# One more buffer for gathered rows, three instead of four groups projected beside the table, and a looser pacing of gathers, in a graph attention layer on one core

## The chip, the cores and the metric

The kernel runs on one core of a Trainium2 chip. The metric is the device time of one execution in microseconds (us), and of several executions the median counts. In this text PE (or TensorE) is the matrix engine and PEld its weight loads, DVE (VectorE) and ACT (ScalarE) are the two elementwise engines, POOL (GpSimd) here does little but start indirect gathers, and SP starts most of the direct transfers.

## The reference

A graph attention layer with a residual, a batch normalization over the nodes and a layer normalization, on 12,500 nodes and 212,500 edges that are sorted by their destination. Cut to what matters:

```python
Q = (x @ WQ).reshape(N, H, dh)          # N = 12500, D = 128, H = 8 heads of dh = 16
K = (x @ WK).reshape(N, H, dh)
V = (x @ WV).reshape(N, H, dh)
Eh = (edge_attr @ WE).reshape(-1, H, dh)
score = K[src] * Q[dst] / jnp.sqrt(jnp.float32(dh)) * Eh
score = jnp.exp(jnp.clip(score.sum(-1, keepdims=True), -5.0, 5.0))
msg = V[src] * score
wV = jax.ops.segment_sum(msg, dst, num_segments=N)
Z = jax.ops.segment_sum(score, dst, num_segments=N)
h = x + (wV / (Z + ATTN_EPS)).reshape(N, D)
h = (h - h.mean(0)) * rsqrt(var(h) + BN_EPS) * gamma + beta
out = layernorm(x + h)
```

Everything is float32.

## The kernel before

**Edges, tiles and groups.** The edges are cut into 1661 tiles of 128 edges, and the tiles into 208 groups of up to 8 (`G`). A group is the unit of the main loop. Its two halves of four tiles each write into one window of 64 destination nodes. The order of the instructions on every engine is the order in which the program is written (`manual_schedule`); no planner moves them. Only waits on data and on buffers decide when they run.

**The table of K and V.** `K[src]` and `V[src]` are rows of a table `kvd` in DRAM, 12,500 rows of 256 numbers (1 KB). The program builds it first: 25 steps of `table_rows` (L656 to L676), each for four blocks of 128 nodes: eight projections with `w_kv` (L663), evacuations that alternate between ScalarE and VectorE (`evac`, L306 and L307), and one write on SP's queue (L671). The first preparations of the main loop (one-hot matrices, queries, edge attributes of groups 0 to 2) are spread over the last steps, written out by hand in the list `steps`. `q_window(w)` reads two node numbers into ScalarE's registers and copies the x columns of the two windows of group w (L497).

**Gathers on POOL.** Groups from 8 (`nxg`) on take their table rows with indirect gathers: one instruction of POOL (L225) for one tile, 128 rows of 1 KB; a group's eight make a set. A set lands in one of 8 slots (`NSLOT`), tiles of the pool `rows`. The list `free` names the free slots and `pending` the groups that still want one; `load_kv` (L279) pairs them and puts the gathers into `queued`. It is called where a slot comes free: after `message(g)` (L603), the last reader of group g's rows, and after the projection of the groups below.

A gather that is queued is issued at one place of an iteration of the main loop: `pace(step)` (L237) issues the first and makes it wait for the product of that iteration that has just been written (`add_x`, L643, or `q_mm`, L528); `issue()` sends the rest behind it.

**The first eight groups.** They can't wait for the table. POOL gathers rows of x for them (64 gathers of 128 rows of 512 bytes), two groups in one slot, called a pair slot here. The rows are transposed (`turn_x`, L322) and projected (`project`, L329) by the kernel itself. `EARLY` = 4 groups are projected beside the table, in two pieces of four tiles each, into slots of their own; the other four in the main loop (`project_main`, L480, with all copies on ScalarE), one per iteration and one iteration ahead of their use, into the table's buffers `t`. Of the x gathers 11 start at once, and the rest are paced by the table: after each step those that are due wait for one of its evacuations (L675).

**Rows fetched on SP.** To relieve POOL, the last tile of 24 groups doesn't come by a gather but by single transfers of one row (1 KB) on SP's queue (`fetch_rows`, L277). There are 3072 of them, spread 16 to an iteration from iteration 8 (`FIRST_ROW`) to 199. On the same queue stand the group's edge attributes `ea` (L477, 512 KB, four iterations ahead) and the node numbers of the one-hot matrices.

**An iteration of the main loop** (L767 to L813) for group g writes in this order: `load(g+4)` of `ea`; `fetch_rows(g)`; `products(g)` (L579, rows times queries); `both_halves(g+1)` (L560); `add_x(g-3)` and `q_mm(g+3)` with the paced gathers; `gather_sum(g-1)` (L618, the segment sums on TensorE); `project_main(g+1)` for the first groups; `turn_back(g+1)` (L568); `scores(g)` (L585); the exponential; `ehqe(g+2)` (L547 the projection of `ea`, L549 its evacuation, L555 the queries); `message(g)` (L603); `onehot(g+1)` (L508). After iteration 7 the table's pool is closed (`tps.close()`), and a new pool `late` takes its memory, for the tiles that the fetched rows land in. After the loop the nodes are normalized and written out.

Of the kernel before, what the change touches and what calls it, by code (L numbers as in the profile page):

```python
# [8 lines left out]
F32 = mybir.dt.float32  # L9
# [8 lines left out]
P = 128  # L18
# [3 lines left out]
G = 8  # L22
# [2 lines left out]
CH = 512  # L25
NSLOT = 8
NX = 8
EARLY = 4
RUN = 64
ROWS = P  # L30
FIRST_ROW = 8
# [51 lines left out]
def gnn_kernel(  # L83
# [33 lines left out]
    rows = ctx.enter_context(tc.tile_pool(name="rows", bufs=1))  # L117
# [6 lines left out]
    late = []  # L124
# [16 lines left out]
    nxg = min(NX, sum(k == G for k in sizes))  # L141
# [9 lines left out]
    def load_xT(upto):  # L151
        while loaded[0] < min(upto, N):
            c = loaded[0]
            n = min(512 if c < 1024 else 1024, N - c)
            nc.sync.dma_start(hx[:, c:c + n], xT[:, c:c + n])
            loaded[0] += n
# [53 lines left out]
    free = list(range(NSLOT))  # L210
    pending = list(range(nxg, NG))
# [1 line left out]
    steady = [False]  # L213

    def slot(i):
        return rows.tile([P, 2 * G * P], F32, name=f"slot{i}")

    def kv_view(g, t):
        SLOT[g] = t[0]
# [9 lines left out]
    queued = []  # L229

    def issue(n=0):
        while len(queued) > n:
            f, *a = queued.pop(0)
            f(*a)
# [13 lines left out]
    for (_, n), groups in zip(ROW_STREAMS, row_plan(usizes)):  # L248
# [6 lines left out]
        if tot % n:  # L255
            q = tot // n
# [22 lines left out]
    def load_kv():  # L279
        while free and pending and table[0]:  # L280
            g = pending.pop(0)
            i = free.pop(0)
            kv_view(g, (i, slot(i)))
            for j in range(sizes[g] - (g in by_row)):
                queued.append((gather, KV[g](j, j + 1, 0, 2 * P).rearrange("p a d -> p (a d)"), kvd,
                               starts[g] + j))
            if not steady[0]:
                issue()
# [46 lines left out]
    def within(f, g):  # L335
        return f(g) if 0 <= g < NG else None


    runs = []
# [151 lines left out]
    def q_window(g):  # L491
        _, BASE[g] = nc.values_load_multi_w_load_instructions(
            base_i[0:1, 2 * g:2 * g + 2], engines=(ET.Activation,), min_val=0, max_val=N,
            skip_runtime_bounds_check_because="node ids")
        XW[g] = wp.tile([P, P], F32, name="xw", bufs=8)
        for h in (0, 1):
            nc.scalar.activation(XW[g][:, h * WN:(h + 1) * WN], hx[:, ds(BASE[g][h], WN)], AF.Copy)  # L497
# [158 lines left out]
    def table_rows(b):  # L656
        t = tab.tile([P, 4, 2 * P], F32, name="t", bufs=4)
        for q in range(b, min(b + 4, NB), 2):
            ps = wide()
            m = min(2, NB - q)  # L660
            for i in range(m):
                n = min(P, N - (q + i) * P)
                nc.tensor.matmul(ps[:n, i, :], hx[:, (q + i) * P:(q + i) * P + n], w_kv, start=True, stop=True)  # L663
            fl = min(m, N // P - q)
            if fl:
                step = evac(t[:, q - b:q - b + fl, :], ps[:, :fl, :])
            if fl < m:
                nc.vector.tensor_copy(t[:n, q - b + fl, :], ps[:n, fl, :])
        full = min(4, N // P - b)
        if full > 0:  # L670
            nc.sync.dma_start(kvd[b * P:(b + full) * P, :].rearrange("(c p) d -> p c d", p=P), t[:, :full, :])  # L671
        if b + 4 > N // P and N % P:
            r0 = N // P * P
            nc.sync.dma_start(kvd[r0:N, :], t[:N - r0, N // P - b, :])
        while len(queued) > max(0, nxg * G - 11 - 11 * (b // 4 + 1) // 5):  # L675
            pace(step)  # L676

    NQ = -(-NB // 4)
    early = min(EARLY, nxg)
    piece = {}  # L680
    for k in range(2 * early):
        piece.setdefault(3 + k * (NQ - 4) // (2 * early), []).append((k // 2, 4 * (k % 2)))
    def both_halves(g):
# [1 line left out]
        both(g, 1)  # L685


    steps = [[(locate,)], [(place, runs[0])], [(q_window, 0), (q_window, 1)], [(q_mm, 0), (q_hi, 0)],
             [(q_mid, 0), (load_rel, 0)], [(q_lo, 0), (load, 0)], [(q_mm, 1), (q_hi, 1), (load_rel, 1)],
             [(q_mid, 1), (q_window, 2)], [(q_lo, 1), (load_rel, 2)], [(load, 1)], [(turned_onehot, 0)],  # L690
             [(turned_onehot, 1)], [], [(ehqe, 0), (both_halves, 0)], [(turn_back, 0), (q_mm, 2), (q_hi, 2)],
             [(q_mid, 2)]]
    first_step = NQ - len(steps) - 1
    assert first_step > 3 and max(piece) < first_step + 14
    for q in range(NQ):
        load_xT((q + 5) * 4 * P)
        if q == 2:
            load_rest()
        for g, a in piece.get(q, []):
            if a == 0:  # L700
                i = free.pop(0)
                kv_view(g, (i, slot(i)))
            turn_x(g, a)
        table_rows(4 * q)
        for g, a in piece.get(q, []):
            project(g, a, wide)
        k = q - first_step
        if 0 <= k < len(steps):
            for f, *a in steps[k]:
                f(*a)  # L710
# [47 lines left out]
    def within_checks(g):  # L758
        if g >= first_check and (g - first_check) % every == 0:
            check((g - first_check) // every)  # L760
# [6 lines left out]
    for g in range(NG - 2):  # L767
        within(load, g + 4)
        within(load_rel, g + 5)
        if (g + 6) % RQ == 0 and (g + 6) // RQ in quads:  # L770
            load_quad((g + 6) // RQ)
        fetch_rows(g)
        within(products, g)
        within(both_halves, g + 1)
        step = within(add_x, g - 3)
        step = within(q_mm, g + 3) or step
        if step is not None and queued:
            pace(step)
        issue()
        within(gather_sum, g - 1)  # L780
        if g + 1 < nxg and g + 1 not in SLOT:
            for _ in project_main(g + 1):
                pass
        within(turn_back, g + 1)
        within(scores, g)
        within(clip_exp, g)
        within(q_hi, g + 3)
        within(x_out, g - 3)
        within(sums_out, g - 1)
        within(q_lo, g + 2)  # L790
        within(denom, g - 2)
        within(recip, g - 2)
        within(attn, g - 2)
        within(q_window, g + 4)
        within(turned_onehot, g + 3)
        within(ehqe, g + 2)
        within(q_mid, g + 3)
        within(message, g)
        within(onehot, g + 1)
        if g == 2:  # L800
            load_last()
        for r in runs[1:]:
            if g == max(4, r[0] // 2 - 12):
                place(r)
        within_checks(g)
        while free and todo and not pending:
            load_x()
        bn_parts(2 * g - 5, 2 * g - 3)
        if g == 4:
            nc.vector.tensor_scalar(row_ids, row_ids, 8 * P, None, op0=OP.mult)  # L810
        if g == FIRST_ROW - 1:
            tps.close()
            late.append(tps.enter_context(tc.tile_pool(name="late", bufs=1)))  # L813
    last = NG - 1
    g = last - 1
    assert not any(k >= g for k in fill)
# [5 lines left out]
    step = add_x(g - 3)  # L822
# [320 lines left out]
```

## Time and profile before

| | |
|---|---|
| median of 3 runs | 2701.23 us (2698.18, 2701.23, 2709.0) |
| the profiled execution, its own time | 2704.18 us |
| its span, first to last instruction | 2702.4 us |
| mean granted TensorE clock | 0.826 |
| PE, DVE, POOL, ACT busy | 71%, 61%, 58%, 24% of the span |
| indirect gathers of table rows on POOL (L225) | 1573, 948 ns each |
| one-row fetches on SP's queue (L277) | 3072, 1 KB each |
| DMA packets, bytes | 177,915; 386.83 MB |

The durations below are those of the profiled execution. A line of a timeline gives the start in us from the span's beginning, the duration in us, the engine, the source line, the operation with its output and inputs, the number of instructions in a row that the line stands for, and in brackets how long the engine was idle before and what released it. `remote` there is a releaser that the profile can't name, and `issue` means that the engine waited for nothing that the profile shows. In a table of costly groups, the columns are busy time with the mean in ns, and then the idle time before, with the wait that ended most of it.

### The profile page before, as it was taken

Reading aid. Unit: us, or ns where it says so; the run is one execution under the profiler, and the core shown is the slowest. Engines: PE = TensorE matmul, PEld = TensorE weight load, DVE = VectorE, ACT = ScalarE, POOL = GpSimd, SP = SyncE. Lnnn points to the kernel's source line nnn. Section 1 sums busy time; section 2 is a strip of 40 time slices with the busy share of each in tenths; the row PEclk is TensorE's granted clock in tenths of the full one; section 3 lists DMA queues with packets and bytes.
Section 4 is the critical chain, followed back from the end, with each engine's and each line's share of the span. In section 5 each row is a group of like instructions: output and inputs, shape, how many; then the busy total and the mean of one; then the engine's idle time right before and its main releaser. Section 6 shows DMA issues by size and latency. Waiting matters only on the chain. (4 is left out here: it accounts for less than half of the span.)

```text
span 2702.4 us, 37686 instructions
## 1 busy us (share of the span) xinstructions
PE 1926.2 (71%) x9414; PEld 1144.2 (42%) x9414; DVE 1644.1 (61%) x3598; ACT 658.4 (24%) x2477; POOL 1579.8 (58%) x1673
## 2 busy tenths in 40 slices
PE   7787766767777767667675767667777767677677
PEld 5454433433434434334333444334344434444446
DVE  3456665565666565666554665656656656656577
ACT  2242222222222222222221222222222222222225
POOL 5645665565666666565654666665656665656624
PEclk8888888887888878888777888878778887878899
DMA  7744444444454444454444544444544444544454
GB/s 225 237 138 139 139 133 143 127 145 135 136 144 141 135 140 141 129 151 130 141 139 117 145 134 135 139 140 130 146 134 140 141 141 132 149 133 140 141 174 127
DMA packets 177915, 386.83 MB, mean 143 GB/s; under 512 B 38864, under 2 KB 94713, under 8 KB 177689
## 3 DMA queue, kind: packets, MB, share of 16 engines
q0 software_dynamic: 77552, 210.48, 26.8%
q1 hardware_dynamic: 95972, 171.08, 20.8%
q10 hardware_dynamic: 4163, 2.79, 0.3%
q8 instruction: 77, 1.26, 0.2%
q14 instruction: 151, 1.22, 0.1%
HBM read 364.58 MB, written 19.63 MB: 142 GB/s over the span
## 5 line engine op out<-in xcount | busy, mean ns | idle before, releaser
L225 POOL DMA_INDIRECT slot<-kvd,srcs x1573 | 1491.1, 948 | 1002.3 <-PE ps_m L528 469.5
L547 PE MATMUL ps_e<-ea,w_e 128*128 128x512 f32 x832 | 640.4, 914 | 528.7 <-DMA ea<-eaT 455.1
L560 DVE TENSOR_TENSOR wt<-wt,ps_q 128x512 f32<-128x512 f32 x416 | 267.6, 682 | 501.1 <-PE ps_q L555 153.5
L618 PE MATMUL ps_a<-msg,oh 128*128 128x136 f32 (+1 forms) x3322 | 516.8, 293 | 9.6 <-issue 8.8
L547 PEld LDWEIGHTS ps_e<-ea,w_e 128*128 128x128 f32 x832 | 207.9, 276 | 738.9 <-issue 719.7
L549 ACT ACTIVATE wt<-ps_e 128x512 f32<-128x512 f32 x416 | 243.1, 595 | 1024.9 <-PE ps_e L547 374.9
L618 PEld LDWEIGHTS ps_a<-msg,oh 128*128 128x128 f32 (+1 forms) x3322 | 415.6, 167 | 88.9 <-issue 61.6
L579 DVE TENSOR_TENSOR p<-slot,ps_t 128x512 f32<-128x512 f32 (+1 forms) x408 | 263.3, 671 | 172.0 <-PE ps_e L547 86.0
L568 PE MATMUL ps_t<-ident,wt 128*128 128x128 f32 x1661 | 248.2, 294 | 130.0 <-DVE wt L560 94.5
L568 PEld LDWEIGHTS ps_t<-ident,wt 128*128 128x128 f32 x1661 | 202.1, 150 | 152.4 <-DVE wt L560 107.3
L585 DVE TENSOR_REDUCE s<-p 128x64 f32<-128x1024 f32 (+1 forms) x209 | 251.7, 1204 | 0.2
L594 ACT ACTIVATE ps_m<-s 128x64 f32<-128x64 f32 (+1 forms) x209 | 47.5, 227 | 823.2 <-DVE s L593 468.7
L603 DVE TENSOR_TENSOR msg<-slot,ps_m 128x1024 f32<-128x1024 f32 (+1 forms) x206 | 243.2, 1182 | 0.6 <-ACT ps_m L594 0.6
L555 PE MATMUL ps_q<-ot,q 64*128 64x512 bf16 x1248 | 220.0, 469 | 0.0
L555 PEld LDWEIGHTS <-q 64*128 64x128 bf16 x1248 | 50.6, 106 | 294.0 <-issue 280.3
L508 DVE TENSOR_TENSOR oh<-ps_m,rel_i 128x512 f32<-128x512 f32 x208 | 141.7, 681 | 10.0 <-remote 8.6
L643 PE MATMUL ps_m<-ident,at 128*128 128x128 f32 x412 | 109.9, 352 | 41.4 <-DVE oh L511 22.3
L643 PEld LDWEIGHTS ps_m<-ident,at 128*128 128x128 f32 x412 | 70.1, 214 | 153.5 <-issue 88.6
L579 DVE TENSOR_TENSOR p<-byrow,ps_t 128x128 f32<-128x128 f32 x24 | 6.9, 286 | 157.7 <-DMA byrow<-kvd 118.2
L497 ACT ACTIVATE xw<-hx 128x64 f32 x416 | 84.1, 248 | 62.3 <-issue 58.0
L648 ACT ACTIVATE hx<-ps_m 128x64 f32 x412 | 90.8, 220 | 11.4 <-PE ps_m L644 3.3
L528 PE MATMUL ps_m<-w_q,xw 128*128 128x128 f32 x416 | 82.8, 282 | 10.3 <-issue 8.6
(167 smaller groups left out, 1625.6 us busy)
## 6 DMA issues: line engine op xcount, KB each, us to landing
ea<-eaT SPq DMA_DIRECT2D x207, 512.0 KB
byrow<-kvd SPq DMA_DIRECT2D x3072, 1.0 KB
slot<-kvd,srcs POOLq DMA_INDIRECT x1573
rbq<-relT SPq DMA_DIRECT2D x94, 256.0 KB
kvd<-t SPq DMA_DIRECT2D x24, 512.0 KB
slot<-xT SPq DMA_DIRECT2D x24, 256.0 KB
out<-o SPq DMA_DIRECT2D x23, 256.0 KB
hx<-xT SPq DMA_DIRECT2D x11, 512.0 KB
```

The source lines that it names most:

```text
L225: return nc.gpsimd.indirect_dma_start(out=out, out_offset=None, in_=table, in_offset=bass.IndirectOffsetOnAxis(ap=srcs[:, e:e + 1], axis=0))
L508: nc.vector.tensor_tensor(one, iota_ps[:, None, :].to_broadcast([P, n, P]), r[:, :n, None].to_broadcast([P, n, P]), op=OP.is_equal)
L547: nc.tensor.matmul(eh, w_e, EA[g][:, a:b, :].rearrange("p a b -> p (a b)"), start=True, stop=True)
L549: nc.scalar.activation(t[:, :(b - a) * P], eh, AF.Copy)
L555: nc.tensor.matmul(QE[g][h], Q3[g][r, k, :], OT[g][r, :(b - a) * P], start=(k == 0), stop=(k == 2))
L560: nc.vector.tensor_tensor(t, t, QE[g][h], op=OP.mult)
L568: nc.tensor.transpose(ps[:, j, :], WT[g][h][:, j * P:(j + 1) * P], ident)
L579: nc.vector.tensor_tensor(PR[g][:, c:d, :], KV[g](c, d, 0), PW[g][i][:, c - a:d - a, :], op=OP.mult)
L585: nc.vector.tensor_reduce(SS[g][:, a:b, :], PR[g][:, a:b, :].rearrange("p t (h d) -> p t h d", d=DH), axis=AX.X, op=OP.add)
L603: nc.vector.tensor_tensor(MSG[g][:, a:b, :P].rearrange("p t (h d) -> p t h d", d=DH), KV[g](a, b, P).rearrange("p t (h d) -> p t h d", d=D ...
L618: nc.tensor.matmul(AGG[g][WN if j >= n else 0:], OH[g][j], MSG[g][:, j, :], start=(j == 0), stop=(j == n - 1))
L643: nc.tensor.matmul(ps, AT[g], ident, start=True, stop=False)
```

## The change

- `EARLY` is 3: group 3 is no longer projected beside the table but in the main loop, like groups 4 to 7. The six pieces that are left are spread over the same steps.
- A ninth slot exists once the table's memory is free: at the end of iteration 7 slot number 8 is allocated from `late[0]`, put into `free`, and `load_kv` is called. Once no group is pending any more, the slot is taken out of `free` again, so that it isn't used for the reload of x at the end.
- The x gathers are paced by 12/5 instead of 11/5 per step of the table.
- The gathers that the main loop queues are paced only from iteration 8 on; before it all are issued without the wait.
- `q_window(0)` and `q_window(1)` are called at the beginning of table step 10 instead of its end, and `q_window(2)` at the beginning of step 16 instead of the end of step 15.

```diff
-EARLY = 4
+EARLY = 3
...
     def slot(i):
-        return rows.tile([P, 2 * G * P], F32, name=f"slot{i}")
+        return (rows if i < NSLOT else late[0]).tile([P, 2 * G * P], F32, name=f"slot{i}")
...
-        while len(queued) > max(0, nxg * G - 11 - 11 * (b // 4 + 1) // 5):
+        while len(queued) > max(0, nxg * G - 11 - 12 * (b // 4 + 1) // 5):
             pace(step)
...
-    steps = [[(locate,)], [(place, runs[0])], [(q_window, 0), (q_window, 1)], [(q_mm, 0), (q_hi, 0)],
+    steps = [[(locate,)], [(place, runs[0])], [], [(q_mm, 0), (q_hi, 0)],
...
-             [(q_mid, 1), (q_window, 2)], [(q_lo, 1), (load_rel, 2)], [(load, 1)], [(turned_onehot, 0)],
+             [(q_mid, 1)], [(q_lo, 1), (load_rel, 2)], [(load, 1)], [(turned_onehot, 0)],
...
+    windows = {first_step + 2: (0, 1), first_step + 8: (2,)}
     for q in range(NQ):
+        for w in windows.get(q, ()):
+            q_window(w)
         load_xT((q + 5) * 4 * P)
...
         step = within(q_mm, g + 3) or step
-        if step is not None and queued:
+        if step is not None and queued and g >= FIRST_ROW:
             pace(step)
         issue()
...
         within_checks(g)
+        if NSLOT in free and not pending:
+            free.remove(NSLOT)
         while free and todo and not pending:
             load_x()
...
         if g == FIRST_ROW - 1:
             tps.close()
             late.append(tps.enter_context(tc.tile_pool(name="late", bufs=1)))
+            free.append(NSLOT)
+            load_kv()
```

## The prediction, made before the changed kernel ran

> **What bounds the kernel now.** I read the page first, then the waits, then the timeline of single engines: SP's queue, POOL, and VectorE's score reductions (L585, one per group, so their starts are a clock of the groups). Page and waits:
>
> ```profile
> L225 POOL DMA_INDIRECT slot<-kvd,srcs x1573 | 1491.1, 948 | 1002.3 <-PE ps_m L528 469.5
> byrow<-kvd SPq DMA_DIRECT2D x3072, 1.0 KB
> PE ps_e L547 <- DMA ea<-eaT: 455.1, 135, 8.2
> ```
>
> No engine is full. TensorE's longest wait is for the edge attributes (`ea`), and those stand on SP's queue behind the 3072 one-row loads, 16 per group, so 192 rounds. SP's queue in the timeline:
>
> ```profile
> 210.89 0.33 SPq L477 DMA_DIRECT2D ea<-eaT  x1
> 214.43 5.24 SPq L277 DMA_DIRECT2D byrow<-kvd  x16
> ...
> 223.69 11.35 SPq L277 DMA_DIRECT2D byrow<-kvd  x16
> ...
> 2605.52 5.49 SPq L277 DMA_DIRECT2D byrow<-kvd  x16
> ```
>
> From the first round (214.4) to the end of the last (2611.0) are 2396.6 us, 12.5 us for each of 192 rounds, and SP issues nearly without pause. So the program is a head of 214 us, 192 rounds, and a tail of 91 us. Whatever moves the start of the first round moves the end by the same amount; what happens beside the rounds counts only if it changes a round.
>
> The same 16 loads take 5.2 us or 11.4 us. POOL tells which:
>
> ```profile
> 106.63 1.01 POOL L225 DMA_INDIRECT slot<-kvd,srcs  x1 [2.76 <-DMA rb<-relT]
> ...
> 135.44 0.95 POOL L225 DMA_INDIRECT slot<-kvd,srcs  x1 [0.30 <-issue]
> 140.88 0.94 POOL L225 DMA_INDIRECT slot<-kvd,srcs  x1 [4.49 <-PE ps_a L618]
> ...
> 149.77 0.94 POOL L225 DMA_INDIRECT slot<-kvd,srcs  x1 [0.30 <-issue]
> ...
> 203.84 0.94 POOL L225 DMA_INDIRECT slot<-kvd,srcs  x1 [15.49 <-PE ps_m L528]
> ...
> 212.60 0.94 POOL L225 DMA_INDIRECT slot<-kvd,srcs  x1 [0.30 <-issue]
> 223.00 0.94 POOL L225 DMA_INDIRECT slot<-kvd,srcs  x1 [9.46 <-PE ps_m L528]
> ...
> 231.76 0.95 POOL L225 DMA_INDIRECT slot<-kvd,srcs  x1 [0.30 <-issue]
> ```
>
> The round at 214.4 lies in POOL's pause from 213.5 to 223.0: 5 us. The one at 223.7 lies under eight gathers (223.0 to 232.7): 11 us. Gathers slow down what runs beside them. Eight take 10 us (140.88 to 149.77 and one more).
>
> A long row of gathers does more than slow down. Without a pause POOL ran from 106.6 to 136.4: 24 gathers, the sets of groups 8, 9 and 10. In that time:
>
> ```profile
> 116.60 1.21 DVE L603 TENSOR_TENSOR msg<-slot,ps_m 128x1024 f32<-128x1024 f32 x1
> 126.42 0.28 ACT L623 ACTIVATE os<-ps_a 128x136 f32<-128x136 f32 x1 [10.06 <-remote]
> 127.85 0.77 PE L528 MATMUL ps_m<-w_q,xw 128*128 128x128 f32 x2 [8.57 <-issue]
> ```
>
> and the score reductions:
>
> ```profile
> 105.19 1.21 DVE L585 TENSOR_REDUCE s<-p 128x64 f32<-128x1024 f32 x1
> 114.26 1.21 DVE L585 TENSOR_REDUCE s<-p 128x64 f32<-128x1024 f32 x1
> 142.29 1.21 DVE L585 TENSOR_REDUCE s<-p 128x64 f32<-128x1024 f32 x1
> 149.72 1.21 DVE L585 TENSOR_REDUCE s<-p 128x64 f32<-128x1024 f32 x1
> 166.21 1.22 DVE L585 TENSOR_REDUCE s<-p 128x64 f32<-128x1024 f32 x1
> 179.45 1.21 DVE L585 TENSOR_REDUCE s<-p 128x64 f32<-128x1024 f32 x1
> 192.36 1.21 DVE L585 TENSOR_REDUCE s<-p 128x64 f32<-128x1024 f32 x1
> 204.82 1.21 DVE L585 TENSOR_REDUCE s<-p 128x64 f32<-128x1024 f32 x1
> 216.47 1.21 DVE L585 TENSOR_REDUCE s<-p 128x64 f32<-128x1024 f32 x1
> 223.98 1.21 DVE L585 TENSOR_REDUCE s<-p 128x64 f32<-128x1024 f32 x1
> ```
>
> Group 1 to group 2 takes 28.0 us where group 0 to 1 took 9.1: 18.9 us are lost, and the groups go on at 139 us, three after the burst. The gathers of x beside the table show the same:
>
> ```profile
> 3.17 1.15 POOL L225 DMA_INDIRECT slot<-x,srcs  x1 [2.01 <-DMA srcs<-src]
> ...
> 23.36 0.94 POOL L225 DMA_INDIRECT slot<-x,srcs  x1 [0.30 <-issue]
> 27.92 0.94 POOL L225 DMA_INDIRECT slot<-x,srcs  x1 [3.62 <-ACT t L306]
> ...
> 97.61 0.94 POOL L225 DMA_INDIRECT slot<-x,srcs  x1 [3.04 <-DVE t L307]
> 19.36 0.60 ACT L306 ACTIVATE xt<-ps_t 128x512 f32<-128x512 f32 x1 [4.42 <-remote]
> 27.06 0.60 ACT L306 ACTIVATE t<-ps_e 128x512 f32<-128x512 f32 x1 [7.10 <-remote]
> 81.39 0.69 DVE L307 COPY t<-ps_q 128x512 f32<-128x512 f32 x1 [4.81 <-remote]
> ```
>
> 17 in a row (3.2 to 24.3) held ScalarE 4.4 + 7.1 = 11.5 us, until 27.1; the stop at 81.4 follows a shorter row. I take this as the rule of the case: about 10 us into a row of gathers the other engines stop, until about 3 us after its end. What the kernel calls pacing keeps sets apart.
>
> **The change, part by part.** The ninth slot. Sets are asked for some seven groups ahead: the 16 sets before the first round's 214 us are eight, for groups 8 to 15, and group 8's scores come at 216.5 although its gathers began at 106.6. No wait of a product for a slot stands among the long waits. Storing one set more ahead therefore hides nothing new: a set is still begun once per group, paced as before from group 8 on. Group 16's set moves one iteration forward, into the pause in which the first SP round took 5.2 us; that round may grow to 11.4 (+6.1), and at the end the gathers finish one iteration earlier, so one late round shrinks by as much. Net 0, ends -6 and +6. Its memory is the table's, free after group 7's message; the pool's other tiles were already placed there.
>
> The q windows. Windows 0 and 1 move from the end of a step of the table to its beginning, on ScalarE; window 2 keeps its place in ScalarE's order. Copies of 0.4 us, ends of -1 and 0; taken as 0.
>
> Three groups beside the table. One group fewer is two pieces fewer, each four transposes and eight products, with three copies on ScalarE or VectorE beside them. The products of one such piece and the share of each engine in the table's middle (us, then PE, PEld, DVE, ACT, POOL; clock, DMA share, GB/s), and a copy of a q window:
>
> ```profile
> 60.42 0.60 PE L322 MATMUL ps_t<-ident,slot 128*128 128x128 f32 x4
> 62.58 1.03 PE L329 MATMUL ps_q<-w_kv,xt 128*128 128x256 f32 x4
> 63.45 1.03 PE L329 MATMUL ps_e<-w_kv,xt 128*128 128x256 f32 x4
> 57.70 0.40 ACT L497 ACTIVATE xw<-hx 128x64 f32 x2 [1.03 <-issue]
> 50.00:100.00 50.00, 45.58 (x201) 36.80 (x202) 18.03 (x31) 15.40 (x34) 27.41 (x29) 0.91 0.82 266
> ```
>
> 2.66 us a piece, 5.3 for both; TensorE was busy 45.6 of the 50 us, so -4.8 if it sets the table's pace. The group is now projected in the loop, all on ScalarE. Groups 3 to 6 carry a projection (their next scores come 16.5, 13.2, 12.9, 12.5 us later, the first still recovering; mean of the last three 12.9), group 7 carries a gather set alone (11.7), and group 8 neither (7.5). So +1.2 if a set lies there too, +5.3 if none does; I take +3.1.
>
> Looser pacing of x. 53 of the 64 gathers are paced, 2.4 instead of 2.2 per step of four blocks; at 1.25 us each that is 3.0 instead of 2.75 us of POOL per step, and they are out two steps before the table ends. Rows of gathers grow longer: I allow three quarters of one more stop like that at 81.4, +3.5; ends 0 (nothing is added) and +9.6 (two stops). Table in sum: -1.3.
>
> No pacing before group 8. The sets of groups 8, 9 and 10 follow each other already. Set 11 waited 4.5 us for the paced matmul, and that pause ended the stop. Without it the slot is free (group 1's message ran at 116.6, before the stop bit), and set 11 follows at once: 32 gathers, 40 us. The stop lasts 10 us longer; beside group 7 a set that stands alone cost 11.65 - 7.51 = 4.1 us, which falls away. +5.9, ends 0 and +10. Then the pair 1 slot comes free in iteration 2 (group 3's projection, now in the loop) and group 2's slot in the same iteration, so sets 12 and 13 run as one row of 20 us instead of two of 10 with a pause. Price by the row nearest in length, the 17 gathers at the start: 11.5 us, less 8.2 for two single sets: +3.3; ends -8 and +11.
>
> Sum: -1.3 + 3.1 + 5.9 + 3.3 = +11.0 us. The profiled execution took 2704.2 us, span 2702.4 and 1.8 around it, 3.0 over the median of 2701.2; so 2715.2 for it, **2712 us** for the median. About 0.5% (13.5 us: 2687.7 and 2714.7) is what a measurement of this kernel tells from no change.
>
> **Rivals.**
> Gathers do not stop the engines. Then rows of any length are free, pacing cost nothing and its loss brings nothing: -4.8 + 3.1, 2699.5 us. This is what the Trainium skill states, in SBUF — State Buffer, section Who interferes with whom: DMA never contends with a compute engine, and PE and ACT never wait on anyone; by that rule alone the sum would have no burst term. The trace disagrees, with 10.06 us on ScalarE inside the 30 us burst. What speaks for this rival otherwise is that the waits end on a releaser the profile can't name; against it, three stops, each beside a row of gathers.
>
> The stop shrinks. From 97.6 us the x gathers ran almost into the kvd sets; in the new order POOL rests for the last two steps of the table. If the stop needs what the earlier gathers left behind, the engines run on longer before it bites: of 18.9 us it could take 14, and -1.7 from the first rival's terms: 2685.5 us. For it: at 116.6 VectorE was still on time, so a few us of delay let group 2 through. Against it: the burst itself gets longer.
>
> A second full stop (slower). Sets 12 and 13 start while the engines have just come back, and stop them as long as the first burst did: 18.9 instead of 11.5, set 11's stop costs its full 10, so -1.3 + 3.1 + 10 + 18.9 - 8.2 = +22.5: 2724 us. It decides from the point where set 13 follows set 12 without a pause while group 3 is still short of its scores. For it: both slots come free in one iteration. Against it: set 12 has to wait for TensorE to return, which gives a pause first.
>
> The change doing nothing it says: for the ninth slot that is my forecast already.
>
> **How the numbers follow.** Forecast 0.42 (0.27 within 0.5%, 0.15 beyond, since its terms reach from 2704 to 2722); first rival 0.14; the stop shrinks 0.23 (0.22 faster); second stop 0.21. Faster 0.22, within 0.5% 0.42, slower 0.36. The range takes in 2685.5 with its lower half cut, and the second stop with a table that got 10 us slower: 2684 to 2734.
>
> **What would show it.** Right: POOL in one row from about 105 to 145 us; group 1 to 2 in some 35 us; sets 12 and 13 in a row with another gap of over 15 us between scores; first SP round starting near 225 instead of 214; rounds of 12.5 us as before and the same tail. Wrong: the first round at 205 or earlier (the stop shrank), or a mean round other than 12.5 us, which would mean that the slot or the shifted sets act on the rounds, a thing for which I have no term: 0.1 us there is 19 us.

## The result, and the profile after

The changed kernel took 2731.58 us (median of 6 runs, 2729.0 to 2737.0), the kernel before 2708.30 us (6 runs, 2698.18 to 2712.51): a ratio of 1.0109, 95% interval 1.0089 to 1.0129. It is slower by about 1%, where 2712 was forecast. The profiled execution took 2731.76 us, 27.6 over the one before. Two of the costly groups on the page of the changed kernel:

```profile
L225 POOL DMA_INDIRECT slot<-kvd,srcs x1573 | 1492.0, 948 | 1018.1 <-issue 417.7
L547 PE MATMUL ps_e<-ea,w_e 128*128 128x512 f32 x832 | 628.5, 898 | 510.3 <-DMA ea<-eaT 478.2
```

The gathers are the same in number and length, and TensorE still waits longest for `ea`. SP's queue in the timeline of the changed kernel, its first and its last round of fetches:

```profile
238.36 10.22 SPq L277 DMA_DIRECT2D byrow<-kvd  x16
...
2628.76 5.54 SPq L277 DMA_DIRECT2D byrow<-kvd  x16
```

The head ends at 238.4 instead of 214.4 us (+23.9), the 192 rounds take 2395.9 instead of 2396.6 us (12.48 us each in both), and the tail takes 95.7 instead of 91.4 us (+4.3). So the division into head, rounds and tail holds, the rounds are untouched, and nearly all of the loss is in the head. Its steps, by the writes of the table (SP's queue, before and then after), the rows of gathers (POOL, after) and the starts of the groups' scores (VectorE, after):

```profile
101.57 0.41 SPq L674 DMA_DIRECT2D kvd<-t  x1
```
```profile
105.91 0.42 SPq L674 DMA_DIRECT2D kvd<-t  x1
```
```profile
109.64 0.95 POOL L225 DMA_INDIRECT slot<-kvd,srcs  x1 [6.76 <-issue]
...
148.54 0.95 POOL L225 DMA_INDIRECT slot<-kvd,srcs  x1 [0.30 <-issue]
156.19 0.94 POOL L225 DMA_INDIRECT slot<-kvd,srcs  x1 [6.71 <-PE ps_t L322]
...
174.95 0.94 POOL L225 DMA_INDIRECT slot<-kvd,srcs  x1 [0.30 <-issue]
194.44 0.94 POOL L225 DMA_INDIRECT slot<-kvd,srcs  x1 [18.55 <-PE ps_t L322]
...
219.78 0.94 POOL L225 DMA_INDIRECT slot<-kvd,srcs  x1 [15.37 <-PE ps_t L322]
...
239.34 0.95 POOL L225 DMA_INDIRECT slot<-kvd,srcs  x1 [9.83 <-PE ps_m L528]
```
```profile
109.51 1.21 DVE L585 TENSOR_REDUCE s<-p 128x64 f32<-128x1024 f32 x1
116.56 1.21 DVE L585 TENSOR_REDUCE s<-p 128x64 f32<-128x1024 f32 x1
156.16 1.21 DVE L585 TENSOR_REDUCE s<-p 128x64 f32<-128x1024 f32 x1
176.55 1.21 DVE L585 TENSOR_REDUCE s<-p 128x64 f32<-128x1024 f32 x1
192.03 1.21 DVE L585 TENSOR_REDUCE s<-p 128x64 f32<-128x1024 f32 x1
...
217.37 1.21 DVE L585 TENSOR_REDUCE s<-p 128x64 f32<-128x1024 f32 x1
...
240.20 1.21 DVE L585 TENSOR_REDUCE s<-p 128x64 f32<-128x1024 f32 x1
```

POOL ran as forecast: one row of 32 gathers (109.6 to 149.5), then a row of 16 (156.2 to 175.9), then single sets behind long pauses. Beside the row of 32 the groups made one step, of 39.6 us; beside the row of 16 again one, of 20.4 us. How an engine stops can be read from TensorE's own timeline in the changed kernel, at the end of the first row:

```profile
147.80 0.37 PE L322 MATMUL ps_t<-ident,slot 128*128 128x128 f32 x1 [2.41 <-issue]
150.60 0.37 PE L322 MATMUL ps_t<-ident,slot 128*128 128x128 f32 x1 [2.43 <-issue]
153.40 0.37 PE L322 MATMUL ps_t<-ident,slot 128*128 128x128 f32 x1 [2.43 <-issue]
154.10 0.37 PE L322 MATMUL ps_t<-ident,slot 128*128 128x128 f32 x1 [0.33 <-issue]
154.81 1.11 PE L322 MATMUL ps_t<-ident,slot 128*128 128x128 f32 x4 [0.33 <-issue]
```

TensorE isn't standing still: it starts one product every 2.8 us, four times the 0.70 us that follows, where the last four of the same line take 1.11 us together. The profile names nothing that it waits for ("issue"). What the other engines wait for is seen earlier in the same row. Here are products of TensorE, and below them instructions of ScalarE and VectorE that wait for such products:

```profile
114.69 2.36 PE L618 MATMUL ps_a<-msg,oh 128*128 128x136 f32 x16
...
117.76 1.88 PE L547 MATMUL ps_e<-ea,w_e 128*128 128x512 f32 x4
...
132.46 0.77 PE L528 MATMUL ps_m<-w_q,xw 128*128 128x128 f32 x2 [12.06 <-DVE oh L508]
```
```profile
131.03 0.28 ACT L623 ACTIVATE os<-ps_a 128x136 f32<-128x136 f32 x1 [12.12 <-remote]
131.03 0.69 DVE L508 TENSOR_TENSOR oh<-ps_m,rel_i 128x512 f32<-128x512 f32 x1 [10.67 <-remote]
153.42 0.60 ACT L549 ACTIVATE wt<-ps_e 128x512 f32<-128x512 f32 x1 [21.34 <-remote]
```

ScalarE copies `ps_a` (L623) at 131.0 us, though the products that fill it (L618) were over, by the profile, at 117.1. VectorE goes on in the same moment (its L508 overwrites one-hot matrices that those products read), and TensorE's next product (L528) waits for VectorE: from 120.4 to 131.0 us none of the three computes. The copy of `ps_e` (L549) starts at 153.4 us, 33.8 us after its products (L547) were over. In the trace each of these three waiting instructions waits for one counter, which finished work of TensorE alone raises. So TensorE had begun its work in time; late is the word that it is done. (The profile models the ends of products, so a late count can't be told from a late last write of the product.) The lines of the prediction show the same in the kernel before: the product that paced set 11 was over at 128.6 us (127.85 and 0.77), but POOL, idle since 136.4, was released at 140.9. In a run of the changed kernel without stops (described below) the copies follow their products at once:

```profile
96.93 1.88 PE L547 MATMUL ps_e<-ea,w_e 128*128 128x512 f32 x4
```
```profile
97.99 0.60 ACT L549 ACTIVATE wt<-ps_e 128x512 f32<-128x512 f32 x1 [0.54 <-PE ps_e L547]
```

Of the 416 copies of L549 in that run none starts more than 1.8 us after its products' end; in the profile before the change the latest is 22.8 us behind, in the one after it 35.2. Three other causes don't fit the stretch from 119 to 156 us. The DMA engines weren't full: they were busy 33% and moved 95 GB/s, nearly all of it gathers, where they were busy 72% at 213 GB/s from 86 to 113 us of the run without stops, in which no group is held up. No packet of the two queues that load instructions lies in that stretch. And the granted clock was 0.60, but a product took 0.37 us there, so a slower clock by itself doesn't put 2.8 us between the starts of two. Why the word comes late beside gathers isn't shown.

### The profile page after: what moved, and what is told of

It reads as the page before. It is cut to its first block, busy times and chain, and to the rows that moved or that the text cites. A ratio compares the mean times of both kernels' runs of the same rounds, so it can differ in the third digit from the quotient of the medians.

```text
span 2730.0 us, 37685 instructions
## 1 busy us (share of the span) xinstructions
PE 1917.0 (70%) x9414; PEld 1141.9 (42%) x9414; DVE 1639.9 (60%) x3596; ACT 662.0 (24%) x2480; POOL 1580.6 (58%) x1673
## 3 DMA queue, kind: packets, MB, share of 16 engines
q1 hardware_dynamic: 95972, 171.08, 21.3%
## 5 line engine op out<-in xcount | busy, mean ns | idle before, releaser
L547 PE MATMUL ps_e<-ea,w_e 128*128 128x512 f32 x832 | 628.5, 898 | 510.3 <-DMA ea<-eaT 478.2
L618 PE MATMUL ps_a<-msg,oh 128*128 128x136 f32 (+1 forms) x3322 | 514.8, 292 | 14.5 <-issue 13.9
L547 PEld LDWEIGHTS ps_e<-ea,w_e 128*128 128x128 f32 x832 | 206.3, 274 | 719.4 <-issue 681.6
L549 ACT ACTIVATE wt<-ps_e 128x512 f32<-128x512 f32 x416 | 244.9, 595 | 991.3 <-PE ps_e L547 406.5
L618 PEld LDWEIGHTS ps_a<-msg,oh 128*128 128x128 f32 (+1 forms) x3322 | 413.1, 166 | 90.8 <-issue 63.0
L568 PE MATMUL ps_t<-ident,wt 128*128 128x128 f32 x1661 | 253.7, 298 | 159.6 <-DVE wt L560 116.0
L585 DVE TENSOR_REDUCE s<-p 128x64 f32<-128x1024 f32 (+1 forms) x209 | 251.5, 1203 | 0.2
L508 DVE TENSOR_TENSOR oh<-ps_m,rel_i 128x512 f32<-128x512 f32 x208 | 141.6, 681 | 12.0 <-remote 10.7
L528 PE MATMUL ps_m<-w_q,xw 128*128 128x128 f32 x416 | 81.8, 279 | 13.6 <-DVE oh L508 12.1
```

The costliest lines, as they stand in the source:

```text
L508: nc.vector.tensor_tensor(one, iota_ps[:, None, :].to_broadcast([P, n, P]), r[:, :n, None].to_broadcast([P, n, P]), op=OP.is_equal)
L547: nc.tensor.matmul(eh, w_e, EA[g][:, a:b, :].rearrange("p a b -> p (a b)"), start=True, stop=True)
L549: nc.scalar.activation(t[:, :(b - a) * P], eh, AF.Copy)
L568: nc.tensor.transpose(ps[:, j, :], WT[g][h][:, j * P:(j + 1) * P], ident)
L585: nc.vector.tensor_reduce(SS[g][:, a:b, :], PR[g][:, a:b, :].rearrange("p t (h d) -> p t h d", d=DH), axis=AX.X, op=OP.add)
L618: nc.tensor.matmul(AGG[g][WN if j >= n else 0:], OH[g][j], MSG[g][:, j, :], start=(j == 0), stop=(j == n - 1))
```

## The experiments

One thing has to be known to read them. The chips showed two conditions. In one the kernel before takes 2700 to 2740 us at a granted clock near 0.82, as above; in the other it takes 2122 to 2126 us at 0.93. The condition goes neither with the kernel nor with the chip: one chip showed the second (2125.93 us) and 22 minutes later the first (2737.02 us). The first is called "with stops" here, the second "without stops". Each ratio is to the kernel before in the same condition on the same chip. Single profiles scatter in the head: the last write of the table as it was before came at 99.3 to 101.6 us in four kernels, and the first round at 214.4 to 218.8 us in the three whose head is that of the kernel before.

**Parts of the change undone** (with stops; the kernel before took 2733.30 us there). The changed kernel wasn't run beside these four, so they are set against its profile above: first round at 238.4 us, ratio 1.0109.

Pacing before iteration 8 put back:
```diff
-        if step is not None and queued and g >= FIRST_ROW:
+        if step is not None and queued:
```


> The changed kernel, with the pacing of gathers back in the iterations before 8. Theory (rows of gathers without a pause stop the engines): the row of 32 gathers breaks into 24 or fewer and 8, sets 12 and 13 part; group 1 to 2 falls from 39.6 us to about 28, group 2 to 3 from 20.4 to about 13; the first fetch round starts near 220 us instead of 238, and the time is about 18 us below the changed kernel's, some 2714 us. Rival (projecting group 3 in the loop is what costs): the first round stays above 234 us and the time within 4 us of the changed kernel's.

Measured: ratio 1.0080 (1.0052 to 1.0109), first round at 230.6 us. The row of 32 became 24 and 8 and group 1 to 2 fell to 29.1 us, as the theory has it. But sets 12 and 13 still came as one row of 16 (158.0 to 177.7 us), beside which group 3 to 4 took 24.5 us; so of the hoped 18 us only 8 in the head came back. The pacing doesn't keep two sets apart when two slots come free in one iteration.

Four groups beside the table again:
```diff
-EARLY = 3
+EARLY = 4
```


> The changed kernel, with four groups projected beside the table as before; no pacing before iteration 8, as in the change. Theory (rows of gathers): the row of 32 gathers stays and group 1 to 2 stays near 38 us, but set 12 now waits for the message of group 2, so there is no second long row and group 2 to 3 falls from 20.4 us to 8 to 10; first round near 225 us, time some 13 us below the changed kernel's. Rival (projecting group 3 in the loop is what costs): first round at 214 to 218 us, time some 22 us below it.

Measured: ratio 1.0130 (1.0094 to 1.0167), first round at 245.1 us, later by 6.7 us, where both sides expected it earlier. The row of 32 stayed (group 1 to 2 40.3 us), group 2 to 3 fell to 7.4 us as expected, but a row of 16 came two groups later (182.9 to 202.6 us) and group 4 to 5 took 25.1 us. The table's last write came at 107.5 us. The projection in the loop therefore isn't the main cost.

The pacing of x as before:
```diff
-        while len(queued) > max(0, nxg * G - 11 - 12 * (b // 4 + 1) // 5):
+        while len(queued) > max(0, nxg * G - 11 - 11 * (b // 4 + 1) // 5):
```


> The changed kernel, with the x gathers paced by 11/5 per table step as before. Theory (looser pacing of x lengthens the rows of gathers beside the table and slows it): the table's last write goes from 105.9 us back to 101 to 102, everything after it comes 4 to 5 us earlier, time some 4 us below the changed kernel's. Rival (the table's 4 us come from the moved pieces and q windows): last write stays at 105 to 106 us, time unchanged.

Measured: ratio 1.0102 (1.0060 to 1.0144), the table's last write at 99.5 us instead of 105.9, 6.4 earlier, so the looser pacing costs more than the 3.5 us of the forecast; 3.4 us of it are left at the first round (234.9), the rest went into the rows behind it (group 2 to 3 23.3 us instead of 20.4).

The ninth slot never given out:
```diff
-            free.append(NSLOT)
-            load_kv()
```


> The changed kernel without the ninth slot: it is never put into the list of free slots. Theory (the slot hides nothing and costs nothing in the head): first round at 238 us as in the changed kernel, rounds of 12.48 us, and the time from the last fetch round to the end 91 to 96 us; time within 5 us of the changed kernel's. Rival (the slot costs the 4 us that the changed kernel's end is longer, 95.7 against 91.4 us after the last fetch): the end at 91 us, time 4 us below. Rival 2 (the slot brings something in the rounds): mean round above 12.55 us, time 10 us or more above the changed kernel's.

Measured: ratio 1.0063 (1.0042 to 1.0084), first round at 238.7 us as in the changed kernel, 91.6 us from the end of the last fetch (2652.5) to the end (2744.1). So the slot does nothing for the head, and costs at the end. The ratio is 0.0046 below the changed kernel's, some 12.6 us, of which the end explains 4; the rest isn't found in the head and would lie in the rounds, of which more below.

**The ninth slot alone**, on the kernel before.
```diff
-        return rows.tile([P, 2 * G * P], F32, name=f"slot{i}")
+        return (rows if i < NSLOT else late[0]).tile([P, 2 * G * P], F32, name=f"slot{i}")
...
+        if NSLOT in free and not pending:
+            free.remove(NSLOT)
...
+            free.append(NSLOT)
+            load_kv()
```


> The kernel before with the ninth slot alone. Theory 1 (the slot hides nothing and costs nothing): time within 0.15% of before, first round at 214 us, 91 us after the last fetch round. Theory 2 (as the kernel without it was 0.46% closer to before than the changed kernel had been: one set of gathers in excess near the end and in the rounds): 0.3 to 0.5% above before, 8 to 14 us, of which 4 us show after the last fetch round (95 us) and the rest in rounds of 12.52 us or more where before has 12.48.

> The kernel before with the ninth slot alone, once more. If this chip shows the stops: theory 1 (nothing hidden, nothing lost) ratio 0.999 to 1.001, 91 us after the last fetch round; theory 2 (one set in excess) ratio 1.003 to 1.005, 95 us after the last fetch round and rounds longer than those of the other three kernels here. If it doesn't: 0.998 as in the first run.

> The kernel before with the ninth slot alone. On a chip with stops: theory 1 (the reload of x starts one iteration earlier and stands ahead of ea on SP's queue: 4 us at the end, nothing else) head at 214 us, 95 us after the last fetch round, ratio 1.0015. Theory 2 (rounds grow too) ratio 1.004 to 1.005. On a chip without: 0.998.

The first two fell on the condition without stops: ratios 0.9983 (0.9974 to 0.9993) and 0.9986 (0.9974 to 0.9998). The third was with stops: 1.0031 (1.0010 to 1.0052), 96.6 us after the last fetch. What is late there is seen on SP's queue, in the kernel before (first, behind its last fetch) and with the ninth slot alone:

```profile
2611.11 0.36 SPq L477 DMA_DIRECT2D ea<-eaT  x1
...
2612.99 1.78 SPq L464 DMA_DIRECT2D slot<-xT  x4
```
```profile
2646.10 5.51 SPq L277 DMA_DIRECT2D byrow<-kvd  x16
2651.98 1.78 SPq L464 DMA_DIRECT2D slot<-xT  x4
2653.86 0.37 SPq L477 DMA_DIRECT2D ea<-eaT  x1
```

The reload of x starts once no group is pending, and with a slot more that is one iteration earlier: 1 MB of x stands ahead of the next group's `ea`. Holding the reload back to iteration 200, one slot per iteration, tests it. Against the kernel with the ninth slot alone:
```diff
-        while free and todo and not pending:
+        if free and todo and not pending and g >= NG - G:
             load_x()
```


> The kernel before with the ninth slot, and the reload of x held to iteration 200, one slot per iteration, where it starts in the kernel before. On a chip with stops: theory 1 (the end's 4 us come from the early reload) 91 us after the last fetch round, ratio 0.999 to 1.001, some 4 us below the ninth slot alone. Theory 2 (rounds) within 2 us of the ninth slot alone. On a chip without stops: 0.998, as the slot takes a pause of 5 us out of POOL's row.

Measured (with stops): ratio 1.0019 (1.0000 to 1.0037), 92.3 us after the last fetch instead of 96.6. The 4 us at the end are explained and taken back; that makes the slot no gain with stops, and without stops this kernel wasn't run. Whether the slot also lengthens the rounds stays open. With stops, on chips where the kernel before takes near 2735 us, five profiles with it show 12.65 to 12.69 us a round and three without it 12.57 to 12.64; on the two chips that have both kinds the difference is 0.08 to 0.12 us, 15 to 23 us over 192 rounds. An estimate from the medians, each less its profile's head and end, leaves less between them: 12.65 to 12.68 us with the slot, 12.60 to 12.65 without. On the chip of the result both kernels have 12.48. So the ratios of these runs may hold something from the rounds, and what a part does to the head is better read from its first round.

**Three groups beside the table alone**, on the kernel before.
```diff
-EARLY = 4
+EARLY = 3
```


> The kernel before with three groups projected beside the table instead of four. On a chip with stops: theory (the moved projection costs 5 us of the iteration that it joins, and the set order changes: sets 10 and 11 need no message any more) group 2 to 3 grows by 5 us or more, the first row of gathers keeps 24 or grows to 32, first round at 218 to 226 us, ratio 1.002 to 1.005; rival (the table gains what the loop loses) first round at 212 to 216 us, ratio 1.000. On a chip without stops POOL's row of gathers sets the end and the ratio is 0.999 to 1.001.

> The kernel before with three groups projected beside the table instead of four, pacing as before. On a chip with stops: theory (the moved projection costs 5 us of the iteration that it joins; sets 8 to 10 have free slots at once, so the row of 24 comes as before, and two slots come free in iteration 2, so a row of 16 follows) first round at 224 to 230 us, like the 229 us of the changed kernel with its pacing back; ratio 1.004 to 1.007. Rival (the table gains what the loop loses) first round at 212 to 216 us, ratio 1.000.

Without stops 1.0012 (1.0001 to 1.0024). With stops 1.0029 (1.0011 to 1.0047): the table's last write came at 96.9 us, 2.4 to 4.7 earlier than in the kernels with the table of before (99.3 to 101.6), near the 4.8 that the two pieces were priced at, and yet the first round came at 226.5 us, 8 to 12 later than in the three profiles with the head of before. Its scores and its second row of gathers:

```profile
109.77 1.21 DVE L585 TENSOR_REDUCE s<-p 128x64 f32<-128x1024 f32 x1
140.64 1.21 DVE L585 TENSOR_REDUCE s<-p 128x64 f32<-128x1024 f32 x1
155.53 1.21 DVE L585 TENSOR_REDUCE s<-p 128x64 f32<-128x1024 f32 x1
179.11 1.21 DVE L585 TENSOR_REDUCE s<-p 128x64 f32<-128x1024 f32 x1
```
```profile
154.55 0.95 POOL L225 DMA_INDIRECT slot<-kvd,srcs  x1 [5.18 <-PE ps_m L528]
```

Group 2 to 3 takes 14.9 us instead of 7.4 (the projection), group 3 to 4 23.6 us beside the row of 16 (154.6 to 174.3). This is the second row by itself: here it comes from three groups beside the table, because the sets then find their slots in another order.

**No pacing before iteration 8 alone**, on the kernel before.
```diff
-        if step is not None and queued:
+        if step is not None and queued and g >= FIRST_ROW:
```


> The kernel before without pacing in the iterations before 8, nothing else changed. If this chip shows the stops: theory (rows of gathers) set 11 joins the row of 24, which becomes 32; group 1 to 2 at 38 to 40 us instead of 28; a second row of 16 later, where two slots come free in one iteration, with a gap between scores of 20 to 25 us; first round at 230 to 236 us, ratio 1.006 to 1.008. Rival (pacing costs as much as it saves): first round at 212 to 218 us, ratio 1.000. If it doesn't: 0.998 to 1.000, as POOL waits less.

It fell on the condition without stops: 1.0003 (0.9991 to 1.0014). By itself it wasn't tried with stops.

**Shorter rows.** If rows of gathers cost the time, splitting the first one should win some back. On the kernel before, at most one set per iteration from the first on:
```diff
-            if not steady[0]:
-                issue()
...
+        left = len(queued)
         if step is not None and queued:
             pace(step)
-        issue()
+        issue(max(0, left - G))
```


> The kernel before, but the gathers of table rows are held back from the first on: in each iteration at most one set of eight is issued, its first gather paced as in the others, so the row of 24 gathers after the table (sets 8, 9, 10) becomes three rows of eight. Theory (rows of gathers stop the engines once they are over about 10 us long, until they end): group 1 to 2 falls from 28.0 us to 12 to 14, no wait of over 8 us on a releaser that the profile can't name, group 8's scores at 203 to 207 us instead of 216.5, first round near 203 us, time 10 to 13 us below before (ratio 0.995 to 0.996). Rival (the stop goes with the work after the table, not with the length of the row): group 1 to 2 stays above 24 us, time within 4 us of before.

> The kernel that issues one set of gathers per iteration from the first on, once more; its first run fell on a chip whose cores showed a granted clock of 0.93 and no stops beside gathers, so it couldn't tell. If this chip shows the stops (before near 2700 us, clock near 0.82): theory (rows over 10 us stop the engines) group 1 to 2 at 12 to 14 us, first round near 203 us, ratio 0.995 to 0.996; rival (the stop goes with the work after the table) group 1 to 2 above 24 us, ratio 0.999 to 1.001. If it doesn't (before near 2120 us): ratio 1.000 as in the first run.

> The kernel that issues one set of gathers per iteration from the first on. On a chip with stops (before near 2700 us): theory (rows over 10 us stop the engines) group 1 to 2 at 12 to 14 us, first round near 203 us, ratio 0.995 to 0.996; rival (the stop goes with the work after the table) group 1 to 2 above 24 us, ratio 0.999 to 1.001. On a chip without (before near 2120 us): 0.999 to 1.000 as in its other runs.

> The kernel that issues one set of gathers per iteration from the first on, once more. On a chip with stops (before near 2700 us): theory (rows over 10 us stop the engines) group 1 to 2 at 12 to 14 us, first round near 203 us, ratio 0.995 to 0.996; rival (the stop goes with the work after the table) group 1 to 2 above 24 us, ratio 0.999 to 1.001. On a chip without (before near 2120 us): 0.999 to 1.000.

Without stops three times no difference: 0.9997 (0.9988 to 1.0007), 0.9993 (0.9983 to 1.0003), 0.9998 (0.9988 to 1.0008). With stops 0.9994 (0.9971 to 1.0016), and this is the run that matters. The start of its second row of gathers, and its scores (L526 and L583 here are L528 and L585 of the other kernels):

```profile
128.82 0.94 POOL L225 DMA_INDIRECT slot<-kvd,srcs  x1 [3.62 <-PE ps_m L526]
```
```profile
112.16 1.21 DVE L583 TENSOR_REDUCE s<-p 128x64 f32<-128x1024 f32 x1
130.70 1.21 DVE L583 TENSOR_REDUCE s<-p 128x64 f32<-128x1024 f32 x1
141.69 1.21 DVE L583 TENSOR_REDUCE s<-p 128x64 f32<-128x1024 f32 x1
156.87 1.21 DVE L583 TENSOR_REDUCE s<-p 128x64 f32<-128x1024 f32 x1
172.82 1.21 DVE L583 TENSOR_REDUCE s<-p 128x64 f32<-128x1024 f32 x1
190.11 1.21 DVE L583 TENSOR_REDUCE s<-p 128x64 f32<-128x1024 f32 x1
```

The first row now ends before 128.8 us, with 16 gathers and not 24 (they begin at 105.5), and the step beside it fell from 28.0 to 18.5 us with it. But the sets that no longer stood in it stood beside the groups after it, which took 11.0, 15.2, 16.0 and 17.3 us; group 8's scores came at 215.6 us (216.5 before), the first round at 216.8. The expectation of 203 us was wrong: here the shorter row only moved the stops. Three rows of eight, as the expectation had them, did not come about, since the first two sets still ran as one row.

The set in two halves, from iteration 8 on too:
```diff
-                nc.tensor.matmul(QE[g][h], Q3[g][r, k, :], OT[g][r, :(b - a) * P], start=(k == 0), stop=(k == 2))
+                step = nc.tensor.matmul(QE[g][h], Q3[g][r, k, :], OT[g][r, :(b - a) * P], start=(k == 0), stop=(k == 2))
+        return step
...
-        issue(max(0, left - G))
+        issue(max(0, left - 4))
...
-        within(ehqe, g + 2)
+        step = within(ehqe, g + 2)
+        if step is not None and queued:
+            pace(step)
+        issue(max(0, left - G))
```


> As the kernel that issues one set per iteration, and the set itself in two halves: four gathers after the products of q_mm, the rest after the last product of ehqe(g+2). Theory A (what gathers hold up is stored up and runs off in short pauses): the 16 one-row loads take 6 to 8 us throughout, rounds of 11.5 to 12.0 us, time 90 to 180 us below before. Theory B (what counts is the number of gathers, not their order): rounds stay at 12.4 to 12.6 us, and only the head's gain of 10 to 13 us is left. Rival (the second wait delays gathers, or the waits for ea grow): rounds above 12.7 us, slower by 30 us or more.

> The kernel that issues a set in two halves, once more. If this chip shows the stops: theory A (what gathers hold up is stored and runs off in short pauses) 16 one-row loads in 6 to 8 us, rounds of 11.5 to 12.0 us, 90 to 180 us below before; theory B (the number of gathers counts, not their order) rounds of 12.4 to 12.6 us and only the head's 10 to 13 us gained; rival (the second wait delays the gathers) rounds above 12.7 us. If it doesn't: 1.000 to 1.002 as in the first run.

Both fell on the condition without stops: 1.0009 (0.9999 to 1.0019) and 1.0004 (0.9994 to 1.0015). What it does with stops wasn't measured.

**The changed kernel once more.**

> The changed kernel once more, on the same chip as the three that follow. Every theory: 1.011 times the time before, some 27 to 30 us over it; first fetch round near 238 us, 95 to 96 us from the last fetch round to the end.

It fell on the condition without stops: 2117.89 us against 2123.14, ratio 0.9978 (0.9969 to 0.9988), so there the same change is a small gain. POOL in this run up to iteration 8, and the pause at the same place in the kernel with only the pacing off (no ninth slot):

```profile
85.75 0.94 POOL L225 DMA_INDIRECT slot<-kvd,srcs  x1 [2.42 <-issue]
...
164.46 0.94 POOL L225 DMA_INDIRECT slot<-kvd,srcs  x1 [0.30 <-issue]
170.75 0.94 POOL L225 DMA_INDIRECT slot<-kvd,srcs  x1 [5.35 <-PE ps_m L528]
```
```profile
176.39 0.95 POOL L225 DMA_INDIRECT slot<-kvd,srcs  x1 [6.14 <-PE ps_m L528]
```

Without stops POOL is the bound: its 1637 gathers stand 1.25 us apart, which is 2046 of the 2115.6 us of the span, and only pauses can be saved. All pauses of over 0.05 us sum to some 11 us in the changed kernel, 10 to 11 with the ninth slot alone, and 15 to 19 in the seven profiles without the slot. With the slot alone POOL has no pause of over 1 us after 161 us, where three groups beside the table alone leave one of 5.4 us at 177.9. In the changed kernel one of 5.35 us remains, so its gain isn't the slot's alone. In this run the groups pass the rows of gathers at their own pace:

```profile
94.60 1.21 DVE L585 TENSOR_REDUCE s<-p 128x64 f32<-128x1024 f32 x1
101.65 1.21 DVE L585 TENSOR_REDUCE s<-p 128x64 f32<-128x1024 f32 x1
113.47 1.21 DVE L585 TENSOR_REDUCE s<-p 128x64 f32<-128x1024 f32 x1
```

Group 1 to 2 took 7.1 us with POOL in one row from 85.8 to 165.4 us, and group 2 to 3, with its projection, 11.8.

## Why the prediction was wrong

**What held.** Head, rounds and tail; the order of POOL's rows (32, then 16); that the slot does nothing in the head; that a group out of the table's steps shortens the table (2.4 to 4.7 us measured, 4.8 forecast). Of the rivals, the slower one came: sets 12 and 13 in one row, a second full stop, 2724 us. That its +22.5 stands so near the 23.3 between the medians is partly luck: its table is 5.6 us too low, its second row and projection (13.8) 2.7 too high, and it has nothing for the end. The likeliest forecast had the right order of events in the head; it mis-sized three terms there and had the path of the ninth slot wrong at the end. By the profiles of before and after:

| term | forecast | measured |
|---|---|---|
| table (last write) | -1.3 | +4.3 |
| set 11 in the first row (group 0 to 2) | +5.9 | +9.6 (46.7 less 37.1) |
| sets 12 and 13 and the moved projection (group 2 to 6) | +6.4 | +11.1 (61.2 less 50.1) |
| groups 6 to 8 | 0, its gain is in the second line | -1.3 (22.8 less 24.1) |
| rounds | 0 | -0.7 |
| end (ninth slot) | 0 | +4.3 |

1. The table: looser pacing of x cost 5 to 6 us (last write at 104.4 to 105.9 in three profiles with it, 99.5 with it undone), not 3.5, within the ends of 0 to 9.6 that the text gave. The moved q windows, taken as 0, may hold some of the rest: 99.5 with them and 96.9 without, in tables that otherwise do the same; against a scatter of 1 to 2 us that isn't settled. Without stops both together moved the last write by no more than 0.5 us (81.5 us in the changed kernel, 81.1 with three groups alone), so what they cost comes with the stops.
2. The first row: the 10 us for eight more gathers were right. The 4.1 us taken off because group 7's set "falls away" were not: groups 6 to 8 won 1.3.
3. The second row: it was priced by the row of x beside the table (11.5 us) less 8.2 us for two single sets. The row's own step was 20.4 us, about its length, where the same step had taken 7.4: +13.0, near the 14.6 forecast for the row and the projection together (the projection's +3.1 was a choice between +1.2 and, by the numbers given, +5.4). But the three steps behind it became shorter by 1.8 us and not by 8.2, since the two single sets had not cost 4.1 us each: before, the steps with a projection took 13.2 and 12.9 us beside a set (to groups 5 and 6) and 12.5 without one (to group 7). A price for work that is hidden was given back as if it were a gain. These 6.4 us are the largest single miss.
4. The end: the forecast followed the slot through POOL's queue alone and took it as 0. The list that it shortens, `pending`, also releases the reload of x onto SP's queue, ahead of `ea`: 4 us.

The rule itself, "about 10 us into a row the other engines stop", is better said as a length: with stops, one group passes per row, and its step lasts about as long as the row. In ten profiles a row of 16 (20 us) stands beside steps of 18.5 to 25.1 us, one of 24 (30 us) beside 28.0 to 30.9, one of 32 (40 us) beside 39.6 to 40.4. And its remedy doesn't follow: splitting the first row moved the stops, and left the head as long as before. And "stop" is too strong: in the lines above, TensorE's products are heard of 14 to 34 us after their end in the profile, and what needs them waits. What the change lost is overlap. It put 48 gathers into two rows in which two groups passed, and left pauses of 18.6, 15.4 and 9.8 us on POOL, where the kernel before had only 15.5 and 9.5. In the new pause of 18.6 us a group was projected that, by the steps in point 3, would have hidden a set.

The rival that gathers do not stop the engines is right in one of the two conditions. Without stops, 64 gathers in a row left a step at 7.1 us; with them TensorE started one product in 2.8 us and ScalarE sat idle for 21.3. The rule of the Trainium skill (SBUF — State Buffer, section Who interferes with whom) that PE and ACT never wait on anyone, which stands there for the ports of SBUF, agrees with the first and not with the second. Whether the ports were free here isn't shown, only that TensorE's counts came late. The rival's -1.7 us has the sign of the -5.2 us measured without stops, but not for its reason: its two terms are those of three groups alone, which measured 1.0012 there, while the slot alone, which it takes as 0, gave -3.2 and -3.7 us.

What makes the two conditions isn't settled. The gathers are equally long in both (948 ns), so POOL isn't slower; the same chip showed both. The granted clock differs (0.82 and 0.93), but whether as cause or as consequence isn't shown.

## What to carry to other kernels

When transfers come in sets, as the gathers here, price a longer row by its own length and by what it no longer runs beside, and don't book as a gain the sets that were hidden. Follow a freed or added buffer through every list that watches it: here one slot more brought a reload forward onto the queue that bounds the kernel. And measure on more than one chip or at more than one time: a change of 1% had the other sign where gathers didn't disturb the engines.

## What the hardware showed that was not expected

Under a long row of gathers, with stops, the word that TensorE's products are done reached the other engines late (ScalarE up to 35 us after their end in the profile), and TensorE's own instructions start in steps of 0.70 us (0.70 and 2.80 in the lines above) though the profile names nothing that they wait for. Without stops the 16 one-row loads on SP take 5.1 us beside gathers, for instance

```profile
231.08 5.12 SPq L277 DMA_DIRECT2D byrow<-kvd  x16
```

in the changed kernel's second run, where the two rounds beside gathers shown above, with stops, took 10.2 and 11.4. The whole kernel before takes 22% less time without stops on the same chip (2125.93 against 2737.02 us).
